# Two graph layers on one core: where the loaded pieces of S are laid out by batch, and who sums the third group's scores

## The chip, the core and the metric

The kernel runs on one core of a Trainium2 chip. Its time is the device time of one execution in microseconds (us), measured several times; below that is compared as a median. A separate execution under the hardware profiler gives the busy times and waits of each engine. The engines are TensorE (PE; its weight loads are PEld), VectorE (DVE), ScalarE (ACT), GpSimd (POOL) and SyncE (SP, which here only issues transfers). All data are float32.

## The reference

There are 16 batches of 1024 nodes with 256 features, and one adjacency matrix `adj` of 1024 x 1024 whose entries are zero except at the edges. Layer 0 is an attention over all nodes with `adj` as a bias. Layer 1 uses `adj` as a weight:

```python
pre_u = jnp.einsum('bud,dk->buk', h_t, W1[:d])
pre_v = jnp.einsum('bvd,dk->bvk', h_t, W1[d:])
hidden = jax.nn.relu(pre_u[:, :, None, :] + pre_v[:, None, :, :] + b1)
S = jax.nn.sigmoid(jnp.einsum('buvk,ko->buvo', hidden, W2)[..., 0] + b2[0])
a_t = jnp.einsum('buv,bud->bvd', S * A_a, h_t)
m_t = jnp.einsum('uv,bud->bvd', A_m, h_t) * h_t
z_t = beta1 * h_t + beta2 * (jnp.einsum('bvd,de->bve', a_t, Wa) + ba) + beta3 * (jnp.einsum('bvd,de->bve', m_t, Wm) + bm)
```

Both `A_a` and `A_m` are `adj`. Since `S` is multiplied by `adj`, its value is needed only at the edges.

## The kernel before

The 16 batches are cut into three groups of 5, 5 and 6 (`GROUPS`; `SIZE[g]` is a group's number of batches). The work has these stages:

1. Layer 0, batch by batch, up to about 1260 us: attention on TensorE (`attend`, L1067), and the two ends of layer 1's edges (`end`, L1105), stored to DRAM as `pu_d` and `pw_d` by node, with the batches of a group side by side. `ha_d` holds h times Wa in the same way. Lists of the edges are made meanwhile.
2. The scores of a group (`scores`, L1279). The edges stand in 135 slots of 128. For a slot GpSimd fetches rows by index (`fetch`, L1226 for `gv`, L1219 for `gu`), VectorE compares them (`compare`, L1255, two instructions a slot), and the result is summed over 272 columns for each batch (`sums`): either by VectorE in one reduction (L1266) or by ScalarE with one accumulating instruction for each batch (L1269). After every part of up to 16 slots ScalarE makes the tanh (`gates`, L1277), VectorE adds one (L1296), and GpSimd scatters each slot's values to `sa_d` in DRAM (`scatter`, L1235): there the batches of a group stand side by side for each pair of nodes. `gv` has 6 buffers in the third group. The first two groups' scores run beside layer 0; the third group's run from about 1330 to 1890 us.
3. The messages of layer 1 (`message`, `product`: L1165, L1185) and, from 1416 us on, the gathers: for a group, a column block `vc` and a row block `c` (8 each), a piece of 128 x 128 pairs is loaded from `sa_d` (`load_sa`, L1339, issued by SP, 7 buffers), laid out by batch by ScalarE (`part_sa`, L1352, tile `apart`, 4 buffers), weighed with `adj` by VectorE in place (`weigh_sa`, L1357), and multiplied with `ha` by TensorE into PSUM (`gather`, L1370, one product for each batch, in two instructions each). The groups are gathered in the order second, first, third, each in 16 halves of four pieces; the messages of the last batches stand between the halves. After a column block VectorE adds the bias (`add_bz`, L1387) and the PSUM result (`finish_z`, L1393), and ScalarE's queue issues the store (`store_z`, L1397).

The third group's gathers can begin only when its scores are all scattered. Each of its six-batch gathers takes its sixth matrix from a tile of its own (`st["rest"]`).

The order of the work on each engine is fixed by a timetable (`Timetable`): every step has a planned time, the steps are emitted in the order of these times, and each engine then runs its instructions in that order. TensorE's steps follow each other with a planned time of 4/2400 us a column; other steps are placed around them. `begins[p]` is the planned start of the gather of piece p, and

```python
        times.at(due, lambda p=p: load_sa(*p))
        times.at(begins[p] - 8.2, lambda p=p: part_sa(*p))
        times.at(begins[p] - 6.0, lambda p=p: weigh_sa(*p))
```

places the copy 8.2 and the weighing 6.0 planned us before it. The load of a piece is planned 4.0 us before the gather seven pieces earlier. In `scores`, the last argument says for which slots the sums are VectorE's: it is true in the third group for every eighth slot (17 of 135), and false otherwise.

Of the kernel before, what the change touches and what calls it, by code (L numbers as in the profile page):

```python
# [10 lines left out]
ALU = mybir.AluOpType  # L11
# [3 lines left out]
P = 128  # L15
# [356 lines left out]
def edge_layers(  # L372
# [36 lines left out]
    nc = tc.nc  # L409
# [3 lines left out]
    NG = len(GROUPS)  # L413
    SIZE = [hi - lo for lo, hi in GROUPS]
# [508 lines left out]
    st = {}  # L923
# [291 lines left out]
    def fetch(g, k):  # L1215
        t, s = SLOTS[k]
        if s == 0:
            gu = st["gu", t] = pools["gath", g].tile([P, SIZE[g] * R], F32, name="gu", bufs=2)
            nc.gpsimd.indirect_dma_start(  # L1219
                out=gu,  # L1220
                out_offset=None,
                in_=pu_d[g],
                in_offset=bass.IndirectOffsetOnAxis(ap=key_u[:, t : t + 1], axis=0),
            )
        gv = st["gv", k] = pools["gath", g].tile([P, SIZE[g] * R], F32, name="gv", bufs=GV[g])
        nc.gpsimd.indirect_dma_start(  # L1226
            out=gv,
            out_offset=None,
            in_=pw_d[g],
            in_offset=bass.IndirectOffsetOnAxis(ap=idx_v[:, t, s : s + 1], axis=0),  # L1230
        )

    def scatter(g, lg, i, k):
        t, s = SLOTS[k]
        dma = nc.gpsimd.indirect_dma_start(  # L1235
            out=sa_d[g],
            out_offset=bass.IndirectOffsetOnAxis(ap=idx_s[:, t, s : s + 1], axis=0),
            in_=lg[:, i, : SIZE[g]],
            in_offset=None,
            bounds_check=N * N - 1,  # L1240
            oob_is_err=False,
        )
        tc.declare_no_dep(dma.ins, group=f"sa{g}", reason="edges of their own")
        tc.add_to_no_dep_group(f"sa{g}", dma.ins)
# [4 lines left out]
    def compare(k, half):  # L1249
        if k in [0, *PARTS] and half == 0:  # L1250
            st["lg"] = dense.tile([P, PARTS[0], MOST], F32, name="lg", bufs=5)
        cols, op = ((slice(0, HALF), ALU.max), (slice(HALF, R), ALU.min))[half]
        mv = by_batch(st["gv", k])[:, :, cols]
        mu = by_batch(st["gu", SLOTS[k][0]])[:, :, cols]
        nc.vector.tensor_tensor(mv, mv, mu, op)  # L1255

    def place_of(k):

        part = next(i for i, end in enumerate(PARTS) if k < end)
        return (PARTS[part - 1] if part else 0), PARTS[part]  # L1260

    def sums(k, js, lg):
        one = by_batch(st["gv", k])
        i = k - place_of(k)[0]
        if len(js) == one.shape[1]:
            nc.vector.tensor_reduce(lg[:, i, : len(js)], one, AX.X, ALU.add)  # L1266
        else:
            for j in js:
                nc.scalar.activation(  # L1269
                    one[:, j, :], one[:, j, :], AF.Copy, accum_out=lg[:, i, j : j + 1]  # L1270
                )

    def gates(g, k, lg):

        k0, k1 = place_of(k)
        part = lg[:, : k1 - k0, : SIZE[g]]
        nc.scalar.activation(part, part, AF.Tanh, bias=b2_h, scale=0.5)  # L1277

    def scores(g, start, end, on_vector):  # L1279

        for k in range(len(SLOTS)):
            time = start + k * (end - start) / len(SLOTS)

            def first(k=k):
                for n in range(AHEAD[g]) if k == 0 else ():
                    fetch(g, n)
                if k + AHEAD[g] < len(SLOTS):
                    fetch(g, k + AHEAD[g])
                for _ in range(min(len(late), 2 if len(late) > PARTS[0] - 4 else 1)):
                    late.pop(0)()  # L1290

            def last(k=k):
                k0, k1 = place_of(k)
                lg = st["lg", k0]
                part = lg[:, : k1 - k0, : SIZE[g]]
                nc.vector.tensor_scalar(part, part, 1.0, None, ALU.add)  # L1296
                late.extend(lambda i=i: scatter(g, lg, i, k0 + i) for i in range(k1 - k0))

            times.at(time - (15.0 if k == 0 else 0.0), first)
            times.at(time + 0.1, lambda k=k: compare(k, 0))  # L1300
            times.at(time + 0.9, lambda k=k: compare(k, 1))
            k0, k1 = place_of(k)
            if k == k0:
                times.at(time + 0.2, lambda k0=k0: st.update({("lg", k0): st["lg"]}))
            summed = lambda js, k=k, k0=k0: sums(k, js, st["lg", k0])
            if on_vector(k):
                times.at(time + 1.7, lambda f=summed: f(range(SIZE[g])))
            else:
                for j in range(SIZE[g]):
                    times.at(time + 2.0 + 0.6 * j, lambda f=summed, j=j: f((j,)))  # L1310
            if k + 1 == k1:
                times.at(time + 5.4, lambda k=k, k0=k0: gates(g, k, st["lg", k0]))
                times.at(time + 6.0, last)
        ended = end + 4.0
        if g + 1 == NG:
            times.at(ended, lambda: [late.pop(0)() for _ in range(len(late))])
        return ended


    def room(g):  # L1320
        return pools["last" if g + 1 == NG else "late"]
# [13 lines left out]
    def load_sa(g, vc, c):  # L1335

        n = SIZE[g]
        sat = st["sat", g, vc, c] = room(g).tile([P, P, n], F32, name="sat", bufs=SA)
        nc.sync.dma_start(  # L1339
            out=sat.rearrange("p v g -> p (v g)"),  # L1340
            in_=sa_d[g].rearrange("(c p v) g -> c p (v g)", p=P, v=N)[
                c, :, vc * P * n : (vc + 1) * P * n
            ],
        )

    def part_sa(g, vc, c):

        sat = st.pop(("sat", g, vc, c))
        apart = st["apart", g, vc, c] = room(g).tile(
            [P, SIZE[g], P], F32, name="apart", bufs=4  # L1350
        )
        nc.scalar.copy(apart.rearrange("p g v -> p v g"), sat)  # L1352

    def weigh_sa(g, vc, c):
        apart = st["apart", g, vc, c]
        a = adj_sb[:, c, vc * P : (vc + 1) * P]
        nc.vector.tensor_tensor(  # L1357
            apart, apart, a.unsqueeze(1).to_broadcast([P, SIZE[g], P]), ALU.mult
        )

    def gather(g, vc, c):
# [108 lines left out]
    times = Timetable()  # L1470
# [199 lines left out]
    begins = {}  # L1670
# [18 lines left out]
    paced = [started[0] + n * (due - started[0]) / NG for n in range(NG)]  # L1689
    paced[NG - 1] = (paced[NG - 1] + started[NG - 1]) / 2  # L1690
    paced = [max(pair) for pair in zip(started, paced)] + [due]
    for g in range(NG):
        ended = scores(g, paced[g], paced[g + 1], lambda k, g=g: g + 1 == NG and k % 8 == 3)
    opened = paced[NG - 1] + 7.0
    assert lead < paced[NG - 1] - 16.0 and opened < when[0], (lead, paced, when[0])
    times.at(
# [19 lines left out]
    for n, (g, c) in enumerate((g, c) for g in order for c in range(C)):  # L1716
# [4 lines left out]
        else:  # L1721
            k, c1 = divmod(n - HA, C)
# [3 lines left out]
    for i, p in enumerate(parts):  # L1726
        due = when[0] - 36.0 + 4.0 * i if i < SA else begins[parts[i - SA]] - 4.0
        if p[0] + 1 == NG:
            due = max(due, ended + 0.1 + 0.01 * i)
        times.at(due, lambda p=p: load_sa(*p))  # L1730
        times.at(begins[p] - 8.2, lambda p=p: part_sa(*p))
        times.at(begins[p] - 6.0, lambda p=p: weigh_sa(*p))
    for i, (g, vc, half) in enumerate(halves):
        if half == 0:
            due = when[0] - 20.0 + 8.0 * i if i < 4 else when[i - 2] + 13.0
# [6 lines left out]
@with_exitstack  # L1742
def tile_graph_layers(ctx: ExitStack, tc: tile.TileContext, *args):
    nc = tc.nc
    I32 = mybir.dt.int32
    hold = ctx.enter_context(tc.tile_pool(name="hold", bufs=1))
    flag = hold.tile([1, 1], I32, name="flag")
    edge_layers(tc, *args, flag)
    over = nc.values_load(
        flag[0:1, 0:1],  # L1750
        min_val=0,
        max_val=1,
        skip_runtime_bounds_check_because="it is a comparison's result",
    )
    with tc.If(over > 0):
        dense_layers(tc, *args)
# [43 lines left out]
```

## Time and profile before

| what | value |
| --- | --- |
| time, median of 3 runs | 2081.45 us (2078.31 to 2083.23) |
| the profiled execution's own time | 2079.83 us |
| its span, first to last instruction | 2078.1 us |
| granted TensorE clock | 0.994 of full speed |
| busy: PE, DVE, ACT, POOL | 97%, 75%, 66%, 55% of the span |
| `part_sa` L1352 | 192 instructions, 264.2 us of ScalarE |
| `weigh_sa` L1357 | 192 instructions, 165.9 us of VectorE |
| `sums` on VectorE L1266 | 17 instructions, 31.5 us |
| `sums` on ScalarE L1269 | 2058 instructions |

How the lines are read. A group's line has the source line, the engine, the operation, the tiles written and read with their shapes (partitions x elements), the count, then after the first bar the busy time in us and the mean ns of one, and after the second bar the idle time of the engine just before them with what ended it. A line of waits has "who waited <- for whom: us in total, times, longest us". A line of stretches has the start and end in us, the length, then for each engine its busy time and (x) the number of instructions, the granted clock, the transfers' share and GB/s. A line of the timeline has start, duration, engine, line, operation and, in brackets, the idle time before it. An answer on one source line gives duration in ns as least/median/most.

### The profile page before, as it was taken

What the parts mean: (1) busy time and instruction counts of PE and PEld (TensorE: products, weight loads), DVE (VectorE), ACT (ScalarE), POOL (GpSimd) and SP (SyncE); (2) the same over time, 40 slices, a digit from 0 to 9 for tenths busy, and PEclk for the clock granted to TensorE, in tenths of its full rate; (3) what the DMA queues carried; (4) which work ended last, traced back from release to release, by engine and by line L of the source; (5) the groups of instructions that cost most, each with busy time, mean ns of one, the idle gap of its engine ahead of it and who ended that gap; (6) DMA issues with size and microseconds to landing.
All of it is one profiled execution on the core that took longest, in us unless ns stands there. A gap on an engine that the chain in (4) does not pass through costs nothing.

```text
span 2078.1 us, 28958 instructions
## 1 busy us (share of the span) xinstructions
PE 2020.4 (97%) x8577; PEld 1554.9 (75%) x8577; DVE 1566.8 (75%) x2348; ACT 1371.5 (66%) x4842; POOL 1142.4 (55%) x974
## 2 busy tenths in 40 slices
PE   8999999999999999999999999899999999999998
PEld 6888887777786868677888886457677667767887
DVE  7798883677777777677878886578888888884554
ACT  4212222577777868587888777577888888885654
POOL 1121221267676777677777777666777677683000
PEclk9999999999999999999999999999999999999999
DMA  6689886788888889789999999999999999996873
GB/s 220 240 311 343 306 323 235 247 268 288 285 273 270 275 288 297 254 299 308 315 297 318 327 308 310 326 401 399 399 400 370 415 414 405 400 383 254 281 230 123
DMA packets 250007, 644.37 MB, mean 310 GB/s; under 512 B 38642, under 2 KB 139762, under 8 KB 247794
## 3 DMA queue, kind: packets, MB, share of 16 engines
q0 software_dynamic: 82016, 348.87, 47.9%
q1 hardware_dynamic: 132002, 259.36, 34.2%
q10 hardware_dynamic: 35824, 34.22, 4.7%
q8 instruction: 69, 1.13, 0.2%
q14 instruction: 96, 0.79, 0.1%
HBM read 479.56 MB, written 162.92 MB: 309 GB/s over the span
## 4 chain that ended last, share of the span: by engine, by line
PE 61%; DVE 11%; DMA 9%; ACT 8%; issue 7%; POOL 3%; ACTq 0%; POOLq 0%; DVEq 0%
PE pv L1067 18%; PE pp L1105 10%; PE pm L1165 10%; PE pzg L1370 6%; DMA gv<-pw_d,idx_v 5%; ACT gv L1269 5%; PE pf L1013 5%; DVE gv L1255 4%; PE pea L1133 4%; PE pzh L1370 3%; PE pz L1185 2%; ACT apart L1352 2%; POOL sa_d L1235 2%; DMA xh<-in_x_dram 1%; POOL gv L1226 1%
## 5 line engine op out<-in xcount | busy, mean ns | idle before, releaser
L1269 ACT ACTIVATE gv<-gv 128x272 f32<-128x272 f32 x2058 | 856.3, 420 | 313.0 <-DVE gv L1255 204.7
L1255 DVE TENSOR_TENSOR gv<-gv,gu 128x680 f32<-128x680 f32 (+1 forms) x810 | 705.8, 909 | 97.5 <-DMA gv<-pw_d,idx_v 95.5
L1226 POOL DMA_INDIRECT gv<-pw_d,idx_v x405 | 497.1, 1227 | 297.9 <-ACT gv L1269 181.5
L1235 POOL DMA_INDIRECT sa_d<-lg,idx_s x405 | 504.1, 1245 | 135.2 <-issue 108.2
L1067 PE MATMUL pv<-feats,eT 128*128 128x257 f32 x2048 | 465.5, 380 | 2.7 <-DVE eT L1054 2.0
L1165 PE MATMUL pm<-adj_sb,xh 128*128 128x512 f32 x1024 | 452.8, 595 | 2.6 <-DVE xh L1081 2.6
L1067 PEld LDWEIGHTS pv<-feats,eT 128*128 128x128 f32 x2048 | 382.9, 190 | 61.8 <-DVE eT L1054 4.2
L1269 ACT ACTIVATION_READ_ACCUMULATOR gv<-gv 128x1 f32 x2058 | 389.7, 189 | 0.0
L1370 PE MATMUL pzg<-ha_g,apart 128*128 128x256 f32 x1536 | 367.5, 382 | 19.0 <-DVE apart L1357 18.5
L1165 PEld LDWEIGHTS pm<-adj_sb,xh 128*128 128x128 f32 x1024 | 194.3, 191 | 222.4 <-issue 219.8
L1370 PEld LDWEIGHTS pzg<-ha_g,apart 128*128 128x128 f32 x1536 | 290.2, 191 | 77.2 <-DVE apart L1357 29.5
L1352 ACT COPY apart<-sat 128x640 f32<-128x640 f32 (+1 forms) x192 | 264.2, 1394 | 78.0 <-PE pzh L1370 35.5
L1357 DVE TENSOR_TENSOR apart<-apart,adj_sb 128x640 f32<-128x640 f32 (+1 forms) x192 | 165.9, 867 | 123.3 <-ACT apart L1352 123.0
L1105 PE MATMUL pp<-wuv,hT 128*128 128x272 f32 x1024 | 250.5, 395 | 6.7 <-ACT end L1119 3.8
L1105 PEld LDWEIGHTS pp<-wuv,hT 128*128 128x128 f32 x1024 | 194.7, 191 | 53.7 <-issue 6.5
L1054 DVE SCALAR_TENSOR_TENSOR eT<-row,col,grown 128x512 f32<-128x512 f32 x256 | 182.8, 745 | 27.5 <-ACT col L1000 26.8
L852 POOL DMA_INDIRECT table_d<-rec,at x52 | 57.4, 1105 | 248.4 <-DVE rec L845 151.8
L1098 ACT COPY hT<-ph 128x512 f32<-128x512 f32 x96 | 55.1, 575 | 101.0 <-PE ph L1087 100.7
L1133 PE MATMUL pea<-wa,hT 128*128 128x256 f32 x512 | 121.0, 379 | 0.0
L1185 PE MATMUL pz<-wm,mT 128*128 128x256 f32 x512 | 115.7, 379 | 0.0
L1013 PE MATMUL pf<-w1T,xT 128*128 128x257 f32 x512 | 114.1, 380 | 0.9 <-DVE xT L971 0.9
L1370 PE MATMUL pzh<-ha_g,apart 128*128 128x256 f32 x384 | 114.2, 379 | 0.0
(179 smaller groups left out, 1589.0 us busy)
## 6 DMA issues: line engine op xcount, KB each, us to landing
sa_d<-zero SPq DMA_DIRECT2D x128, 512.0 KB, 5.6
sat<-sa_d SPq DMA_DIRECT2D x128, 320.0 KB, 9.5
sat<-sa_d SPq DMA_DIRECT2D x64, 384.0 KB, 4.2
pu_d<-end SPq DMA_DIRECT2D x64, 272.0 KB, 4.3
pw_d<-end SPq DMA_DIRECT2D x64, 272.0 KB, 5.8
ha_d<-ea SPq DMA_DIRECT2D x64, 256.0 KB, 4.9
zb_d<-zb ACTq DMA_DIRECT2D x64, 256.0 KB, 7.8
xh<-in_x_dram SPq DMA_DIRECT2D x15, 1024.0 KB, 13.6
```

Source lines behind the costliest of these rows:

```text
L1013: nc.tensor.matmul(pfs[i], lhsT=st["xT"][:, h, c * P : (c + 1) * P], rhs=w1T[:, h, :], start=(h == 0), stop=(h == H - 1),)
L1054: nc.vector.scalar_tensor_tensor(st["eT", b, k, n][:, i, :], st["row"][:, cols], st["col"][:, j : j + 1], grown[:, j, cols], ALU.max, ALU. ...
L1067: nc.tensor.matmul(pv[:, : D + 1], lhsT=st["eT", b, k, j // 4][:, j % 4, i * P : (i + 1) * P], rhs=st["feats", b][:, j, :], start=(j == 0) ...
L1105: nc.tensor.matmul(pp[:, k, :R], lhsT=st["hTi", b, i][:, h, k * P : (k + 1) * P], rhs=wuv[:, side, h, :], start=(h == 0), stop=(h == H - 1),)
L1133: nc.tensor.matmul(pp[:, k, :], lhsT=st["hTi", b, i][:, h, k * P : (k + 1) * P], rhs=wa[:, h, :], start=(h == 0), stop=(h == H - 1),)
L1165: nc.tensor.matmul(pm, lhsT=held[b][:, c, h * P : (h + 1) * P], rhs=adj_sb[:, c, span], start=(c == 0), stop=(c == C - 1),)
L1226: nc.gpsimd.indirect_dma_start(out=gv, out_offset=None, in_=pw_d[g], in_offset=bass.IndirectOffsetOnAxis(ap=idx_v[:, t, s : s + 1], axis=0),)
L1235: dma = nc.gpsimd.indirect_dma_start(out=sa_d[g], out_offset=bass.IndirectOffsetOnAxis(ap=idx_s[:, t, s : s + 1], axis=0), in_=lg[:, i, : ...
L1255: nc.vector.tensor_tensor(mv, mv, mu, op)
L1269: nc.scalar.activation(one[:, j, :], one[:, j, :], AF.Copy, accum_out=lg[:, i, j : j + 1])
L1352: nc.scalar.copy(apart.rearrange("p g v -> p v g"), sat)
L1370: nc.tensor.matmul(st["pzg", g, vc][j // 4][:, j % 4, :], lhsT=apart[:, j, :], rhs=ha, start=(c == 0 and j % 2 == 0), stop=(c == C - 1 and ...
```

## The change

The step `part_sa` goes away. `weigh_sa` takes the loaded piece, in which the batches of a group are the innermost dimension, reads it by batch (so with a step of 5 or 6 floats from one element to the next), multiplies it with `adj` and writes `apart` in order. It is planned 6.6 us before the gather, where the copy was planned 8.2 and the weighing 6.0 us before it. The tile `apart` is now first written by VectorE, and the loaded piece `sat` is released by it. In the third group all slots' sums go to ScalarE.

```diff
-    def part_sa(g, vc, c):
+    def weigh_sa(g, vc, c):
 
         sat = st.pop(("sat", g, vc, c))
         apart = st["apart", g, vc, c] = room(g).tile(
             [P, SIZE[g], P], F32, name="apart", bufs=4
         )
-        nc.scalar.copy(apart.rearrange("p g v -> p v g"), sat)
-
-    def weigh_sa(g, vc, c):
-        apart = st["apart", g, vc, c]
         a = adj_sb[:, c, vc * P : (vc + 1) * P]
         nc.vector.tensor_tensor(
-            apart, apart, a.unsqueeze(1).to_broadcast([P, SIZE[g], P]), ALU.mult
+            apart,
+            sat.rearrange("p v g -> p g v"),
+            a.unsqueeze(1).to_broadcast([P, SIZE[g], P]),
+            ALU.mult,
         )
...
     for g in range(NG):
-        ended = scores(g, paced[g], paced[g + 1], lambda k, g=g: g + 1 == NG and k % 8 == 3)
+        ended = scores(g, paced[g], paced[g + 1], lambda k: False)
...
-        times.at(begins[p] - 8.2, lambda p=p: part_sa(*p))
-        times.at(begins[p] - 6.0, lambda p=p: weigh_sa(*p))
+        times.at(begins[p] - 6.6, lambda p=p: weigh_sa(*p))
```

## The prediction

> **What bounds the kernel now.** I read the page's busy shares first, then stretches of time, then what TensorE waits for, then rows for single instructions.
>
> ```profile
> PE 2020.4 (97%) x8577; PEld 1554.9 (75%) x8577; DVE 1566.8 (75%) x2348; ACT 1371.5 (66%) x4842; POOL 1142.4 (55%) x974
> ```
>
> TensorE is busy 97% of the span; only 58 us of 2078.1 are idle. The change touches nothing before the third group's scores, so I look at the stretch from the first gather (L1370) to the end of these scores, and at the one after it:
>
> ```profile
> core 0: us, PE busy (x) PEld busy (x) DVE busy (x) ACT busy (x) POOL busy (x), PEclk, DMA share, GB/s
> 1410.00:1885.00 475.00, 456.01 (x1797) 332.51 (x1796) 402.49 (x465) 407.04 (x1361) 341.44 (x251) 1.00 1.00 391
> 1895.00:2070.00 175.00, 175.00 (x812) 154.07 (x811) 89.71 (x92) 97.42 (x64) 0.00 (x0) 1.00 0.73 245
> ```
>
> In the first, TensorE idles 19 us of 475, while VectorE and ScalarE are both some 85% busy and the transfers are full. In the second, TensorE has no idle time: nothing done there can gain, and VectorE has 85 us to spare. In the first stretch, the waits are:
>
> ```profile
> PE pzg L1370 <- DVE apart L1357: 18.5, 23, 2.9
> DVE apart L1357 <- ACT apart L1352: 43.4, 40, 5.5
> DVE gv L1255 <- DMA gv<-pw_d,idx_v: 15.7, 9, 4.3
> DVE lg L1296 <- ACT lg L1277: 12.9, 6, 6.2
> DVE zb L1195 <- PE pz L1185: 1.0, 1, 1.0
> ```
>
> So what there is to gain is 18.5 us at most, all of it TensorE waiting for the weighed piece; behind that VectorE waits for ScalarE's copy. VectorE's sum closes: 402.5 busy + 43.4 for copies + 29.6 for the rest = 475.5.
>
> **The change, part by part.** The rows, one shape each:
>
> ```profile
> L1352 ACT COPY apart<-sat 128x640 f32<-128x640 f32 x128 | 166.8, 1320 | 0.8 <-PE pzh L1370 0.8
> L1352 ACT COPY apart<-sat 128x768 f32<-128x768 f32 x64 | 97.4, 1541 | 77.2 <-PE pzh L1370 34.6 <-DMA sat<-sa_d 23.1 <-DVE apart L1357 19.4
> L1357 DVE TENSOR_TENSOR apart<-apart,adj_sb 128x640 f32<-128x640 f32 x128 | 104.7, 822 | 43.7 <-ACT apart L1352 43.4
> L1266 DVE TENSOR_REDUCE lg<-gv 128x6 f32<-128x1632 f32 x17 | 31.5, 1851 | 0.3
> ```
>
> *Removed from ScalarE:* 192 copies, 264 us; of these 126 (164 us) lie in the first stretch, the last 64 (97 us) where TensorE is full, worth nothing.
> *Moved to ScalarE:* 17 reductions become 17x6 = 102 sums. Sums follow each other every 0.41 us in the timeline (starts at 1500.27, 1500.68, 1501.09), so 42 us in all; the 14 reductions inside the stretch make 84 sums, 34 us. ScalarE goes from 407 to 407 - 164 + 34 = 277 of 475 us: no bound any more.
> *Removed from VectorE:* 14 x 1.85 = 25.9 us in the stretch.
> *Added to VectorE:* the weighing now reads its first operand with a step of 5 floats (20 bytes), or 6 in the third group. No row has a tensor_tensor with such a read, so I bound it. From below: no extra cost, 0.82 us as now (the row's 640 elements take 0.15 us + 640 x 1.04 ns). No reason admits a gain: the same count passes. The nearest VectorE row is a small reduction that reads with a step of 9 floats, beside one that reads in order:
>
> ```profile
> L795 DVE TENSOR_REDUCE end<-short x1: 271/271/271, 68.9 to 68.9; 128x9 f32<-128x63 f32 x1
> L762 DVE TENSOR_REDUCE pieces<-reach x1: 258/258/258, 58.2 to 58.2; 128x9 f32<-128x99 f32 x1
> ```
>
> 99 elements in order take 258 ns, so 63 would take 258 - 36 x 1.04 = 220; the strided one takes 271: 0.8 ns more for each element. The nearest large row is ScalarE's own copy, which writes with a step of 128 floats: (1541 - 1320)/128 = 1.73 ns an element, where its copies in order cost (1001 - 575)/512 = 0.83 (L969 and L1098, 1024 and 512 elements): twice. So the extra per piece of 640 lies between 0, 0.51 us (640 x 0.8) and 0.667 us (a second cycle each). I take 0.667, 1.49 us a piece: the row of like size says exactly double, and the small one errs low if some of its start is hidden. From above, a third cycle would add another 0.667.
>
> [...]
>
> *The sum for the stretch.* VectorE: 402.5 - 25.9 + 127 x 0.667 = 461.3 us, in place of 402.5; TensorE needs 456. The waits for the copy (43.4) go. The other 29.6 stay or shrink: ScalarE's tanh (12.9) will come earlier. All kept: 461.3 + 29.6 = 490.9, that is +16 on 475; none kept: 461.3, -14. With the small row's price VectorE needs 441.6, and the ends are -4 and, by TensorE's own 456, -19.
>
> To place it between -14 and +16 I look where VectorE has no room, since its order is fixed and work cannot move from a full stretch to a loose one:
>
> ```profile
> 1425.00:1575.00 150.00, 133.51 (x154) 1.00 1.02 395
> 1600.00:1650.00 50.00, 46.18 (x53) 1.00 1.03 413
> 1725.00:1850.00 125.00, 113.04 (x130) 1.00 1.02 395
> ```
>
> (VectorE busy.) With 40, 15 and 36 weighings and 5, 2 and 4 reductions in them, they become 133.5 - 9.25 + 26.7 = 151.0, 46.2 - 2.5 + 10.0 = 53.7 and 113.0 - 7.4 + 24.0 = 129.6: over by 1.0, 3.7 and 4.6, together 9.3 us; 6.0 us of waits for other things than the copy lie there, of which I keep half: 12.3. In the rest of the stretch VectorE keeps room (1650 to 1725 comes to 63 of 75 us); there TensorE idled 9.2 us, and with the copy gone I give back half: -4.6. Net +7.7, taken as +8.
>
> *New waits on VectorE.* It now waits itself for the piece to land and for TensorE to free one of four apart buffers (ScalarE's 0.8 us in the first stretch). In a run of gathers TensorE takes 2.16 us each, so the buffer is free 3 x 2.16 = 6.5 us before the gather, and the weighing is due 6.6 before: 0.1 us. Queued behind such a wait are the compares, behind them ScalarE's sums, behind them the gv buffers that GpSimd's fetches need. One transfer (ACT gv <- sat, 6.5 us, once) will hold VectorE instead. SP's load of the next piece waits for the weighing's end, due at -6.6 + 1.49 = -5.1 against the copy's -8.2 + 1.32 = -6.9; the load is due at -4.0, so nothing moves unless VectorE is over 1.1 us late. GpSimd's queue is moved past nothing; ScalarE's stores stand behind fewer instructions.
>
> *What I cost at nothing.* ScalarE's 34 us: covered by 198 us of room. GpSimd's 251 issues take 1.36 us here and 0.97 where VectorE stands idle (1886 to 1892): 99 us in excess, which VectorE's instructions seem to cause. With 341 + 53 us of issue it has 80 us of room; that cover goes only if the excess nearly doubles. The last stretch: 89.7 + 64 x 0.8 = 141 of 175 us, so TensorE stays full. Between them:
>
> ```profile
> 1891.21 0.97 POOL L1235 DMA_INDIRECT sa_d<-lg,idx_s  x1 [0.30 <-issue]
> 1893.65 1.27 SPq L1339 DMA_DIRECT2D sat<-sa_d  x3
> 1898.97 0.96 DVE L1357 TENSOR_TENSOR apart<-apart,adj_sb 128x768 f32<-128x768 f32 x1 [3.52 <-ACT apart L1352]
> 1904.50 1.89 PE L1370 MATMUL pzg<-ha_g,apart 128*128 128x256 f32 x8
> ```
>
> The third group's first piece is ready at 1899.9, its gather begins at 1904.5: 4.6 us of cover, 0.8 more without the copy. If the scores do not end earlier, no gain over some 5 us can come through.
>
> **Rivals.** *Faster (full rate):* VectorE needs 376.6, TensorE's 18.5 us of waits fall to some 4 if the scores end earlier with it: -14, 2067. For it: 43.4 us of VectorE's waits go with the copy. Against: both strided rows. The small row's price with a third of the other waits kept (441.6 + 9.9 = 451.5, under TensorE's 456) ends near it. *No change:* double price, but two thirds of the other waits go, as VectorE runs later than whatever it waited for: 461.3 + 9.9 = 471, within 4 us of 475. *GpSimd takes over (slower still):* if its excess doubles, 341 + 99 + 53 = 493, +18, with VectorE's lateness on top +30: 2111. A third cycle an element would be 127 x 1.333 = 169 on VectorE, 546: +71 at least; unlikely. That the change does not do what it says I rule out: both engines' instruction lists change as stated.
>
> **How the numbers follow.** The profiled execution took 2079.83 (span 2078.1), 1.6 under the median of 2081.45; the change in time is put on the median: 2081.5 + 8 = 2089.5. Forecast 0.48 (own range 2086 to 2100), faster 0.26, no change 0.16, GpSimd or a dearer read 0.10. Below 0.2% (4.2 us) a measurement of this kernel cannot tell it from no change. The range runs from 2066 to 2112. Faster 0.26, same 0.16, slower 0.58.
>
> **What would show it.** L1357 near 1.49 us (640) and 1.75 (768): right; near 0.82: the faster rival. VectorE over 95% busy in the first stretch and ScalarE under 60%: right. "PE pzg <- DVE apart" above 18.5 us, near 26: right; below 10: wrong. L1235 and L1226 above 1.6 us: GpSimd's rival. The last stretch should keep its 175 us; if it grows, I have missed a wait there.

## The result, and the profile after

The changed kernel takes 2146.6 us (2142.98 to 2152.64), the kernel before 2081.45: a ratio of 1.032, 95% interval 1.0306 to 1.0334. It is slower, by 65 us. Its profiled execution took 2152.64 us (span 2150.9, clock 0.982). In the changed kernel the weighing is L1353, the gather L1369, the bias L1386, the PSUM sum L1392; the lines of `scores` keep their numbers.

The page's busy shares, then the stretch from the first gather to the end of the third group's scores and the one after it (start and end, length, busy us and instructions of PE, PEld, DVE, ACT and POOL, clock, transfers):

```profile
PE 2044.5 (95%) x8577; PEld 1566.7 (73%) x8577; DVE 1632.6 (76%) x2331; ACT 1179.1 (55%) x4854; POOL 1260.7 (59%) x974
```

```profile
1416.00:1945.00 529.00, 467.34 (x1768) 337.09 (x1768) 430.58 (x443) 304.80 (x1389) 451.36 (x243) 0.95 0.94 348
1972.00:2138.00 166.00, 162.95 (x744) 141.73 (x743) 124.55 (x91) 0.00 (x0) 0.00 (x0) 0.99 0.74 251
```

The last stretch is nearly as full as before (TensorE is busy 163 of 166 us). The first took 475 us and takes 529, and VectorE is no fuller in it (81%, before 85%). TensorE's granted clock is 0.95 there, 1.00 before, and it is busy 467 us instead of 456; but it also idles 62 us, and GpSimd's account below fills the stretch without it. The engine that grew is GpSimd: 341 us for 251 issues before, 451 for 243 now. An issue is here the GpSimd instruction that starts a fetch or a scatter. Its two main groups in the stretch of before:

```profile
L1235 POOL DMA_INDIRECT sa_d<-lg,idx_s x124 | 169.0, 1363 | 38.4 <-issue 32.9 <-DVE gv L1255 1.2 <-DMA gv<-pw_d,idx_v 0.9
L1226 POOL DMA_INDIRECT gv<-pw_d,idx_v x110 | 151.0, 1373 | 87.9 <-ACT gv L1269 61.1 <-issue 16.2 <-ACT apart L1352 4.5
```

Groups of instructions and waits in the stretch of after:

```profile
L1353 DVE TENSOR_TENSOR apart<-sat,adj_sb 128x640 f32<-128x640 f32 x121 | 159.0, 1329 | 0.0
L1235 POOL DMA_INDIRECT sa_d<-lg,idx_s x116 | 235.0, 2026 | 36.2 <-issue 30.5 <-DMA sa_d<-lg,idx_s 1.5 <-DMA gv<-pw_d,idx_v 1.2
L1226 POOL DMA_INDIRECT gv<-pw_d,idx_v x110 | 183.7, 1670 | 36.5 <-issue 28.3 <-DMA sa_d<-lg,idx_s 2.6 <-ACT gv L1269 2.5
```

```profile
ACT gv L1269 <- DVE gv L1255: 154.0, 54, 9.8
DVE gv L1255 <- DMA gv<-pw_d,idx_v: 94.0, 31, 10.2
...
PE pzg L1369 <- DVE apart L1353: 51.9, 29, 5.4
```

The strided weighing costs 1.33 us instead of 0.82 and waits for nothing. A scatter takes GpSimd 2.03 us instead of 1.36, a fetch 1.67 instead of 1.37, and GpSimd hardly waits for another engine any more (2.5 us for ScalarE's sums, 61.1 before): what is left before its issues is nearly all "issue", 0.30 us each. Its 451 us and 243 x 0.30 = 73 fill 524 of 529. VectorE waits 94 us (15.7 before) for the rows that GpSimd fetches late, and behind those compares stand the weighings that TensorE then waits for: 51.9 us instead of 18.5.

From the start of the first gather to the end of the last scatter, two events that the trace dates in every kernel, the sum closes. Before, 1416.0 to 1892.2; after, 1422.3 to 1965.9:

```profile
1963.66 0.97 POOL L1235 DMA_INDIRECT sa_d<-lg,idx_s  x1 [0.31 <-issue]
1964.94 0.97 POOL L1235 DMA_INDIRECT sa_d<-lg,idx_s  x1 [0.30 <-issue]
```

(A stretch of the timeline, GpSimd's last two issues of after.) The window grew from 476.2 to 543.6 us, its start came 6.3 later (it scatters between 1412.5 and 1424.0 in the kernels below that ran where before takes 2080 us), and what follows the last scatter took 185.9 and 185.0: 67.4 + 6.3 - 0.9 = 72.8, the difference of the two spans. The time of this kernel is the end of the last scatter and 185 us.

This table has that window for all kernels below, worked out from their traces: its length, VectorE's busy time in it, the mean and the longest GpSimd issue, and GpSimd's issues with 0.30 us added to each. Some 253 issues lie in every window (189 in half_scatter).

| kernel | ratio to before (95%) | window us | VectorE us | issue mean, longest us | GpSimd with 0.30 each, us |
| --- | --- | --- | --- | --- | --- |
| before | 1 | 476.2 | 399 | 1.36, 6.0 | 421 |
| after | 1.032 (1.0306 to 1.0334) | 543.6 | 434 | 1.83, 13.6 | 539 |
| only_stride | 1.0314 (1.026 to 1.0369) | 546.0 | 459 | 1.82, 14.0 | 538 |
| only_sums | 0.9975 (0.9966 to 0.9985) | 467.3 | 376 | 1.32, 5.8 | 412 |
| one_input | 1.0031 (1.0019 to 1.0042) | 484.2 | 432 | 1.56, 7.8 | 468 |
| half_scatter | 1.0176 (1.0149 to 1.0204) | 506.1 | 431 | 2.18, 14.7 | 468 |
| weigh_twice | 1.0307 (1.0287 to 1.0328) | 538.6 | 500 | 1.28, 2.2 | 402 |
| stride_out | 1.01 (1.0083 to 1.0116) | 498.7 | 421 | 1.64, 11.9 | 489 |
| split | 1.0264 (1.0244 to 1.0285) | 536.0 | 442 | 1.79, 18.9 | 529 |
| stride_pe | 1.0004 (0.9985 to 1.0024) | 469.4 | 372 | 1.33, 8.9 | 411 |
| extra_step1 | 1.0131 (1.0052 to 1.021) | 503.4 | 458 | 1.22, 2.2 | 384 |
| extra_step2 | 1.0135 (1.0055 to 1.0216) | 504.0 | 458 | 1.22, 2.2 | 384 |
| extra_step4 | 1.0238 (1.0158 to 1.0318) | 527.0 | 489 | 1.28, 4.8 | 399 |
| extra_step5 | 1.026 (1.0171 to 1.035) | 527.6 | 489 | 1.27, 3.8 | 394 |
| extra_free1 | 1.0155 (1.0113 to 1.0196) | 515.5 | 450 | 1.54, 8.1 | 466 |
| extra_free5 | 1.0273 (1.0236 to 1.0311) | 536.2 | 478 | 1.67, 10.8 | 497 |
| after_gap | 0.9999 (0.9988 to 1.0011) | 476.6 | 453 | 1.38, 2.8 | 425 |
| mix_half | 0.9933 (0.9913 to 0.9953) | 461.1 | 375 | 1.34, 8.7 | 416 |

Ratios are to runs of the kernel before on the same chip; where the extra_step kernels and extra_free1 ran, it took 2103 to 2105 us.

### The profile page after: what moved, and what is told of

Its sections match the earlier page's. It is cut to its first block, busy times and chain, and to the rows that moved or that the text cites. A ratio compares the mean times of both kernels' runs of the same rounds, so it can differ in the third digit from the quotient of the medians.

```text
span 2150.9 us, 28917 instructions
## 1 busy us (share of the span) xinstructions
PE 2044.5 (95%) x8577; PEld 1566.7 (73%) x8577; DVE 1632.6 (76%) x2331; ACT 1179.1 (55%) x4854; POOL 1260.7 (59%) x974
## 4 chain that ended last, share of the span: by engine, by line
PE 55%; DMA 15%; DVE 10%; issue 9%; POOL 7%; ACT 3%; POOLq 0%; SPq 0%; DVEq 0%; ACTq 0%
PE pv L1067 16%; PE pm L1165 10%; DMA gv<-pw_d,idx_v 9%; PE pp L1105 8%; PE pzg L1369 5%; PE pf L1013 4%; DVE gv L1255 4%; PE pea L1133 4%; POOL sa_d L1235 3%; POOL gv L1226 3%; PE pz L1185 2%; PE pzh L1369 2%; ACT gv L1269 2%; DVE apart L1353 2%; DMA sa_d<-lg,idx_s 2%
## 5 line engine op out<-in xcount | busy, mean ns | idle before, releaser
L1269 ACT ACTIVATE gv<-gv 128x272 f32<-128x272 f32 x2160 | 898.4, 419 | 467.6 <-DVE gv L1255 301.5
L1255 DVE TENSOR_TENSOR gv<-gv,gu 128x680 f32<-128x680 f32 (+1 forms) x810 | 707.9, 911 | 185.9 <-DMA gv<-pw_d,idx_v 181.4
L1226 POOL DMA_INDIRECT gv<-pw_d,idx_v x405 | 526.7, 1301 | 256.1 <-ACT gv L1269 131.9
L1235 POOL DMA_INDIRECT sa_d<-lg,idx_s x405 | 579.9, 1432 | 134.6 <-issue 111.3
L1165 PE MATMUL pm<-adj_sb,xh 128*128 128x512 f32 x1024 | 457.6, 600 | 13.1 <-DVE mT L1176 9.0
L1369 PE MATMUL pzg<-ha_g,apart 128*128 128x256 f32 x1536 | 381.4, 393 | 55.2 <-DVE apart L1353 52.2
L1269 ACT ACTIVATION_READ_ACCUMULATOR gv<-gv 128x1 f32 x2160 | 407.7, 189 | 0.0
L1369 PEld LDWEIGHTS pzg<-ha_g,apart 128*128 128x128 f32 x1536 | 297.8, 196 | 120.1 <-DVE apart L1353 72.6
L1353 DVE TENSOR_TENSOR apart<-sat,adj_sb 128x640 f32<-128x640 f32 (+1 forms) x192 | 265.4, 1399 | 50.2 <-PE pzh L1369 31.2
L1219 POOL DMA_INDIRECT gu<-pu_d,key_u x63 | 88.7, 1409 | 65.1 <-PE pv L1067 41.0
L1369 PE MATMUL pzh<-ha_g,apart 128*128 128x256 f32 x384 | 117.2, 388 | 0.0
```

The lines of the kernel that those rows point to most:

```text
L1165: nc.tensor.matmul(pm, lhsT=held[b][:, c, h * P : (h + 1) * P], rhs=adj_sb[:, c, span], start=(c == 0), stop=(c == C - 1),)
L1226: nc.gpsimd.indirect_dma_start(out=gv, out_offset=None, in_=pw_d[g], in_offset=bass.IndirectOffsetOnAxis(ap=idx_v[:, t, s : s + 1], axis=0),)
L1235: dma = nc.gpsimd.indirect_dma_start(out=sa_d[g], out_offset=bass.IndirectOffsetOnAxis(ap=idx_s[:, t, s : s + 1], axis=0), in_=lg[:, i, : ...
L1269: nc.scalar.activation(one[:, j, :], one[:, j, :], AF.Copy, accum_out=lg[:, i, j : j + 1])
L1353: nc.vector.tensor_tensor(apart, sat.rearrange("p v g -> p g v"), a.unsqueeze(1).to_broadcast([P, SIZE[g], P]), ALU.mult,)
L1369: nc.tensor.matmul(st["pzg", g, vc][j // 4][:, j % 4, :], lhsT=apart[:, j, :], rhs=ha, start=(c == 0 and j % 2 == 0), stop=(c == C - 1 and ...
```

## The experiments

The expectations call theories by letters. G: GpSimd's issues, held up by VectorE, pace the stretch. R (the moved sums) and S (VectorE's own time) are the first rivals to it. P, fitted to the first four runs: the stretch lasts as long as VectorE's instructions with two operands in SBUF and some 0.40 us for each of GpSimd's issues; the "port" in its name is the author's guess at a cause, and no run shows one. T: the step of the access itself holds GpSimd; the "line" in extra_step1's expectation is likewise an assumption that no run shows. N, which the last runs test, is explained at its place.

### One half of the change each

**only_stride**: the changed kernel, with the 17 reductions left on VectorE.

```diff
-        ended = scores(g, paced[g], paced[g + 1], lambda k: False)
+        ended = scores(g, paced[g], paced[g + 1], lambda k, g=g: g + 1 == NG and k % 8 == 3)
```

> The strided weighing alone; the 17 reductions of the third group stay on VectorE. Theory G (GpSimd's queue is the bound: its transfers' issues are held while VectorE runs instructions with two operands in SBUF, and the longer weighing holds them more): GpSimd's issues stay at 1.75 to 1.9 us in the stretch of gathers and scores, the time is 2130 to 2150 us. Theory R (what cost the time is that all sums are ScalarE's, so that the compared rows come free later): issues fall to some 1.4 us, time 2080 to 2095 us. Theory S (VectorE's own longer busy time): slower than the changed kernel by the 26 us of reductions that come back, 2160 to 2175 us.

**only_sums**: the same edit the other way round, in the kernel before.

> The sums alone: ScalarE makes the copy as before and all sums of the third group; VectorE weighs in place as before. G: VectorE loses 17 instructions with one operand, GpSimd's issues stay within 0.1 us of 1.36, time 2078 to 2092 us (ScalarE goes from 407 to some 441 of 475 us). R: 2110 to 2140 us.

only_stride takes 2145.0 us, as long as the whole change; only_sums takes 2074.9, less than either kernel. So the weighing's half of the change makes the whole loss, and the moved sums are a small gain of their own.

### Less of the suspected load

**one_input** makes the layout on VectorE with the same strided read, but with one operand (a reduction over an axis of length 1); it leaves out the product with `adj`.

```diff
-        nc.vector.tensor_tensor(
...
+        nc.vector.tensor_reduce(
+            apart, sat.rearrange("p v g -> p g v").unsqueeze(3), AX.X, ALU.add
+        )
```

> The strided weighing is replaced by a reduction over a dimension of one element: the same strided read of the piece, the same 640 or 768 results in order, but no second operand (the product with adj is left out). The instruction is expected to take within 0.15 us of 1.33 us. G: GpSimd's issues fall below the 1.36 us of before, to 1.1 to 1.3 us, and the time to 2062 to 2085 us. If it is the stride that disturbs GpSimd, or VectorE's own time (S): issues stay near 1.86 us, or the time stays at 2130 to 2150 us.

**half_scatter**: the changed kernel without every second slot's scatter in the third group.

```diff
     def scatter(g, lg, i, k):
+        if g + 1 == NG and k % 2:
+            return
```

> The changed kernel, but every second slot of the third group is not scattered (67 of GpSimd's issues left out, and their values with them). G: GpSimd's queue loses 67 x 2.3 us = 154 us in the stretch and is no bound any more: time 2070 to 2095 us. S or R: GpSimd is not the bound, time 2130 to 2150 us.

one_input's instruction is as long as the strided weighing, and almost the whole loss is gone (2085.5 us), though the issues, at 1.56 us, stay longer than the 1.1 to 1.3 us that G expected. From its groups of instructions:

```profile
L1353 DVE TENSOR_REDUCE apart<-sat 128x640 f32<-128x640 f32 x124 | 162.3, 1323 | 0.4 <-DMA sat<-sa_d 0.4
```

So neither VectorE's time (432 us in the window, 434 in after) nor the strided read alone is the cause; that the instruction reads two operands matters. half_scatter won half the loss back (2116.9 us), which no theory had said: GpSimd had 64 issues fewer, and those left became longer (2.18 us).

### Two-operand time, the side of the step, shorter instructions, the step on TensorE

**weigh_twice**: the kernel before with the in-place weighing made twice, so that `adj` goes in squared.

```diff
+        nc.vector.tensor_tensor(
+            apart, apart, a.unsqueeze(1).to_broadcast([P, SIZE[g], P]), ALU.mult
+        )
```

> The kernel before with the weighing issued twice, in order and in place (the output then holds adj squared): no stride on VectorE, only more time in instructions with two operands in SBUF. Theory P (port: the stretch lasts as long as VectorE's time in two-operand instructions plus some 0.40 us for each GpSimd issue, whatever the stride; in the runs so far 376.6 + 251 x 0.39 = 475 before, 430.6 + 243 x 0.41 = 529 changed, 432.9 + 188 x 0.39 = 507 with half the scatters): 376.6 + 99 + 100 = 576, 101 us more than before, 2165 to 2195 us, and GpSimd's issues rise above 1.8 us. Theory T (the step in the read disturbs GpSimd): issues stay near 1.36 us. If VectorE's busy time alone is the bound: 402.5 + 99 and 30 of other waits, 2110 to 2145 us.

**stride_out**: the changed kernel, reading `sat` in order and writing `apart` with a step of 128 floats.

```diff
-            apart,
-            sat.rearrange("p v g -> p g v"),
-            a.unsqueeze(1).to_broadcast([P, SIZE[g], P]),
+            apart.rearrange("p g v -> p v g"),
+            sat,
+            a.unsqueeze(2).to_broadcast([P, P, SIZE[g]]),
```

> As the changed kernel, but VectorE reads the piece in order and writes apart with a step of 128 floats. If a strided write costs VectorE what a strided read does (1.3 us): P and T both say 2135 to 2155 us. If it is free (0.82 us): P says 376.6 + 100 = 477 us for the stretch and, with ScalarE relieved, 2065 to 2082 us. T says the same.

**split**: the changed kernel, each weighing cut into two instructions, of two batches and of the rest.

```diff
+        for lo, hi in ((0, 2), (2, SIZE[g])):
...
+                apart[:, lo:hi, :],
+                by[:, lo:hi, :],
+                a.unsqueeze(1).to_broadcast([P, hi - lo, P]),
```

> The changed kernel with each weighing cut into two instructions, two batches and then the rest. P: VectorE gains some 0.1 us a piece, 13 us in the stretch, and nothing is freed: 2150 to 2175 us. If instead GpSimd is let in at the end of an instruction (theory E), more ends mean shorter issues: below 1.65 us on the mean, 2100 to 2130 us.

**stride_pe**: no layout at all: VectorE weighs in order, and TensorE takes its columns with a step of 5 or 6 floats.

```diff
-                lhsT=apart[:, j, :],
+                lhsT=apart[:, :, j],
```

> No layout by batch at all: VectorE weighs the piece in order, without ScalarE's copy, and TensorE takes each batch's matrix from it with a step of 5 or 6 floats as its weights. P: VectorE's weighing is back at 0.82 us, the stretch at 477 us or, TensorE permitting, a little less: 2065 to 2085 us, if the weight load stays at 0.19 us. If the strided load costs twice (0.38 us, where a product starts every 0.216 us): 2048 x 0.16 = 336 us more, some 2400 us.

weigh_twice ends P. Its waits and groups between 1415 and 1880 us:

```profile
POOL gv L1226 <- ACT gv L1269: 124.3, 52, 5.2
...
PE pzg L1373 <- DVE apart L1360: 53.6, 41, 4.1
```

```profile
L1226 POOL DMA_INDIRECT gv<-pw_d,idx_v x101 | 121.2, 1200 | 151.0 <-ACT gv L1269 124.3 <-issue 6.7 <-ACT apart L1352 6.1
```

VectorE is busy 500 of 538.6 us, most of it on two operands, more than in any other kernel here; yet a fetch takes 1.20 us and GpSimd waits 124 us. It is slow because VectorE is full, not GpSimd. stride_out had nearly the changed kernel's instruction length (1.29 us) and lost a third as much: 2101.9 us, where both theories said 2135 to 2155. split shows that the length of the instruction is not the point: pieces of 0.62 and 0.86 us, issues of 1.79; its 2135.2 us lie between what P and E expected. stride_pe is even with before: VectorE back at 0.82 us a piece, no copy, issues 1.33 us; its weight loads pay instead, from 190 to 310 ns, of which little shows in the time: what follows the last scatter takes 190.7 us, 185.9 before (first the group of before, then of stride_pe, in the last stretch):

```profile
L1370 PEld LDWEIGHTS pzg<-ha_g,apart 128*128 128x128 f32 x509 | 96.7, 190 | 13.2
```

```profile
L1366 PEld LDWEIGHTS pzg<-ha_g,apart 128*128 128x128 f32 x501 | 117.5, 310 | 0.0
```

### The price of the step, and whether the step holds GpSimd

**extra_step1, extra_step2, extra_step4, extra_step5**: the kernel before, with one more product of 320 of the weighed elements after each weighing, written over the spent piece, read with a step of s floats.

```diff
+        nc.vector.tensor_tensor(
+            extra.rearrange("p (s v) -> p s v", s=s),
+            flat.rearrange("p (v s) -> p s v", s=s),
+            adj_sb[:, c, :320].rearrange("p (s v) -> p s v", s=s),
+            ALU.mult,
+        )
```

> The kernel before, with one more instruction on VectorE after each weighing: the product of 320 floats of apart with 320 of adj, written over the piece that is no longer needed. Here it reads apart in order. Expected 0.48 us each, VectorE some 54 us busier in the stretch. Theory T (a step of a line or more in VectorE's read holds GpSimd's issues): they stay between 1.25 and 1.4 us; time 2085 to 2115 us. Theory D (it is VectorE's time in instructions with two operands): they rise to 1.45 us or more.

> The same, reading the same 320 floats of apart with a step of 2 floats (8 bytes). T: as in order, 0.48 to 0.6 us each and issues at 1.25 to 1.45 us; time 2085 to 2120 us. D: issues as with step 1.

> The same with a step of 4 floats (16 bytes). T: 0.7 to 0.8 us each, issues at 1.55 us or more; time 2110 to 2150 us. D: issues no higher than its time asks for, within 0.1 us of the run with step 1.

> The same with a step of 5 floats (20 bytes), as the changed kernel has it. T: as step 4, 0.7 to 0.8 us each, issues at 1.55 us or more, time 2110 to 2150 us; if the harm grows with the step, more than step 4. D: within 0.1 us of the run with step 1.

The added product's group in the four kernels: s = 1 and 2 (the same line in both), then 4, then 5:

```profile
L1363 DVE TENSOR_TENSOR sat<-apart,adj_sb 128x320 f32<-128x320 f32 x192 | 94.7, 493 | 6.6
```

```profile
L1363 DVE TENSOR_TENSOR sat<-apart,adj_sb 128x320 f32<-128x320 f32 x192 | 143.6, 748 | 6.6
```

```profile
L1363 DVE TENSOR_TENSOR sat<-apart,adj_sb 128x320 f32<-128x320 f32 x192 | 143.2, 746 | 6.6
```

A step of 8 bytes costs nothing here (493 ns, as in order); at 16 and 20 bytes it costs (748 - 493) / 320 = 0.80 ns an element, which the weighing itself shows too: (1329 - 822) / 640 = 0.79. But all four have issues of 1.22 to 1.28 us, and their ratios (1.0131, 1.0135, 1.0238, 1.026) go with VectorE's added time. T falls.

### Breaks in VectorE's chain

What the slow kernels share shows in the timeline. A stretch of it in the changed kernel, first VectorE, then GpSimd (start, duration):

```profile
1524.03 0.71 DVE L1176 TENSOR_TENSOR mT<-pm,hT 128x512 f32<-128x512 f32 x1
1524.63 1.94 DVE L1255 TENSOR_TENSOR gv<-gv,gu 128x816 f32<-128x816 f32 x2
1526.46 1.36 DVE L1353 TENSOR_TENSOR apart<-sat,adj_sb 128x640 f32<-128x640 f32 x1
1527.71 1.96 DVE L1255 TENSOR_TENSOR gv<-gv,gu 128x816 f32<-128x816 f32 x2
1529.54 2.62 DVE L1353 TENSOR_TENSOR apart<-sat,adj_sb 128x640 f32<-128x640 f32 x2
```

```profile
1525.23 7.70 POOL L1226 DMA_INDIRECT gv<-pw_d,idx_v  x1 [0.30 <-issue]
1533.23 1.01 POOL L1235 DMA_INDIRECT sa_d<-lg,idx_s  x1 [0.30 <-issue]
```

Each of VectorE's seven instructions from 1524.63 on starts some 0.1 us before the one ahead of it ends (1526.46 against 1526.57), so between two of them there is no gap; the chain ends at 1532.16. The fetch issued at 1525.23 ends at 1532.93, 0.77 us after that end. Counted so over the whole windows: a *break* is a place where VectorE's chain of instructions with two SBUF operands stops: a gap, or an instruction with an operand in PSUM or with one operand. An issue is counted as let in at a place if it ends 0.76 to 1.06 us after the VectorE instruction there ends, and as not let in if it goes on longer:

| kernel | at a break | first place without a break | later ones | mean issue us |
| --- | --- | --- | --- | --- |
| before | 62 of 62 | 107 of 114 | 0 of 16 | 1.36 |
| stride_pe | 50 of 50 | 112 of 117 | 0 of 22 | 1.33 |
| weigh_twice | 93 of 93 | 86 of 87 | none | 1.28 |
| extra_step5 | 98 of 98 | 87 of 90 | 0 of 1 | 1.27 |
| after | 69 of 69 | 69 of 113 | 12 of 87 | 1.83 |
| split | 55 of 56 | 73 of 123 | 24 of 163 | 1.79 |

At a break an issue gets in nearly always. Without one it gets in at the first place that it meets or hardly at all, and then waits for the chain's end. In before, VectorE waits for the copy ahead of 40 weighings; in weigh_twice and the extra_step kernels the second of two instructions needs the first, which leaves 0.03 us of gap; in the changed kernel VectorE's instructions mostly wait for nothing and do not depend on each other. That GpSimd's issues are let in for certain only at breaks is theory N, and three runs test it from both sides.

The table shows two differences between before and after, not one. The windows have 119 breaks in before and 87 in after; and at the first place without a break the share let in falls from 107 of 114 to 69 of 113. Lost breaks alone do not make the loss: stride_pe has 91 and keeps the high share.

**after_gap**: the changed kernel with a break behind each weighing, one element multiplied by 1 in place.

```diff
+        one = apart[:, 0, 0:1]
+        nc.vector.tensor_scalar(one, one, 1.0, None, ALU.mult)
```

> The changed kernel with one element of each weighed piece multiplied by 1 in place right after the weighing: an instruction on one operand that depends on the one before it, so that VectorE's unbroken chain of two-operand instructions ends at every weighing. Theory N (GpSimd's issue is let in for certain only where VectorE's chain of two-operand SBUF instructions breaks; in the changed kernel nothing breaks it for 5 to 19 us): the mean issue in the third group's stretch falls from 1.87 us to 1.25 to 1.40, none over about 4.5 us is left, GpSimd's busy time falls from 451 to 310 to 350 us and it waits again; VectorE gains some 127 x 0.15 = 19 us; the time falls from 2145 to 2080 to 2110 us. Rival (the strided read holds GpSimd by what it takes of SBUF, whatever stands between the instructions): the mean issue stays at 1.75 us or more, and the time at 2140 to 2165.

**extra_free5**: extra_step5 without the dependence: the added product reads `adj` only.

```diff
-            flat.rearrange("p (v s) -> p s v", s=5),
+            adj_sb[:, (c + 1) % C, :320].rearrange("p (v s) -> p s v", s=5),
```

> The kernel before with one more VectorE product of 320 floats after each weighing, read with a step of 20 bytes as in extra_step5, but of adj by adj: it does not depend on the weighing, so that no gap stands between the two. It writes over the spent piece and changes no output. Theory N: without the gap the issues are let in less often: mean issue above 1.35 us (extra_step5 had 1.25), tails over 3 us come back; time 2155 to 2180 us on a chip with 2105 for the kernel before, 2130 to 2160 on one with 2080. Rival (a strided read of SBUF does it only in long pieces, or only on a tile that a DMA has written): mean issue 1.20 to 1.30 us and the ratio of extra_step5, 1.017 to 1.035.

**extra_free1**: the same with s = 1.

> As extra_free5, with the added product read in order (0.49 us instead of 0.74): independent of the weighing, no gap, no step. If the missing gap alone keeps GpSimd's issues out, they take 1.5 us or more, as in extra_free5 (1.70). If it needs both, a missing gap and a strided read in the chain (kernels without a strided read let an issue in at the first boundary that it meets in some 95 of 100 cases, gap or not), they take 1.25 to 1.40. Time in both cases by VectorE: ratio 1.008 to 1.025.

after_gap has more VectorE work than the changed kernel and takes 2080.1 us, ratio 0.9999: the whole loss is gone. The stretch of its timeline, VectorE and GpSimd, and the groups between 1415 and 1880 us:

```profile
1605.94 1.34 DVE L1353 TENSOR_TENSOR apart<-sat,adj_sb 128x640 f32<-128x640 f32 x1
1607.32 0.15 DVE L1360 TENSOR_SCALAR apart<-apart 128x1 f32<-128x1 f32 x1
1607.40 1.93 DVE L1255 TENSOR_TENSOR gv<-gv,gu 128x816 f32<-128x816 f32 x2
```

```profile
1606.24 1.88 POOL L1235 DMA_INDIRECT sa_d<-lg,idx_s  x1 [0.31 <-DVE gv L1255]
1608.42 1.73 POOL L1226 DMA_INDIRECT gv<-pw_d,idx_v  x1 [0.30 <-issue]
```

```profile
L1235 POOL DMA_INDIRECT sa_d<-lg,idx_s x119 | 168.5, 1416 | 41.8 <-issue 29.3 <-DVE lg L1296 6.3 <-DVE gv L1255 3.0
L1226 POOL DMA_INDIRECT gv<-pw_d,idx_v x109 | 151.4, 1389 | 74.2 <-ACT gv L1269 42.7 <-issue 17.8 <-DVE gv L1255 6.3
```

The scatter waits through the weighing, which ends at 1607.28, and is done at 1608.12, 0.84 us later, though the compares run on. No issue is longer than 2.8 us, and GpSimd waits for ScalarE again, 42.7 us. Its window has 155 breaks. VectorE is busy 454.5 of 470 us between 1415 and 1885; after_gap has nothing to spare there and does not beat before.

From the other side, taking the gap out of extra_step5 made its issues longer, from 1.27 to 1.67 us, and extra_free1 against extra_step1 from 1.22 to 1.54. So here the missing gap does it without any step (109 breaks in extra_free1, 220 in extra_step1); the step adds to it. Their times moved little (1.026 to 1.0273, 1.0131 to 1.0155, with intervals that overlap): in both GpSimd has room left, and still waits for ScalarE, 41 us in extra_free5 and 46 in extra_free1.

### A version that beats both

**mix_half**: the sums on ScalarE; in the first two groups every second piece as in stride_pe, the others and the third group with the copy.

```diff
+    def plain(g, c):
+        return g + 1 < NG and c % 2 == 1
...
+                lhsT=apart[:, :, j] if plain(g, c) else apart[:, j, :],
```

> A version meant to beat both: all sums of the third group's scores on ScalarE, and of the first two groups' pieces every second one without the copy: VectorE weighs it in order (0.82 us) and TensorE reads its columns with a step of 5 floats (0.309 us a weight load against 0.190); the other pieces and the third group keep ScalarE's copy. Both theories: ScalarE at some 350 us instead of 441 in the stretch, VectorE at 380, GpSimd's issues at 1.3 us; the kernel with the sums alone moved took 0.9975 of before, this one 0.992 to 0.999: 2064 to 2078 us where before takes 2080.

It takes 2067.6 us, ratio 0.9933 (0.9913 to 0.9953), and its profiled run's window is 461 us; TensorE is busy 455.71 of it:

```profile
1424.00:1885.00 461.00, 455.71 (x1801) 356.43 (x1800) 374.58 (x445) 372.80 (x1460) 340.05 (x254) 1.00 1.00 397
```

## Why the prediction was wrong

The sign was right, the size was not: +8 us forecast, +65 measured, above the range's upper end of 2112. The sign was luck: the +8 came from a VectorE that has no room, and with the price that was measured the prediction's own sum puts VectorE at 441 us, under TensorE's 456, and its ends at -4 and -19.

- **The read's price** was too high by a third: 0.667 us forecast for a piece of 640, 0.507 measured. The small reduction's row (0.8 ns an element) was the right neighbour; I chose the copy of another engine, against rows of it that read other tiles (`pt` and `ph`, which TensorE writes). The 1.04 ns an element that stands for one cycle in the prediction is the rate in order of the compares of before (862 ns for 680 elements, 1004 for 816). A third cycle, 1.333 us more for a piece, showed in no run. The runs put the edge between a step of 8 bytes (493 ns for 320 floats) and one of 16 (748), and the price at 0.80 ns an element.
- **VectorE's sum** was close: with the measured price it is 402.5 - 25.9 + 127 x 0.507 = 441, and 431 to 434 was found. It was not the bound: "VectorE over 95% busy" failed: 81%.
- **The step that failed** is GpSimd under "What I cost at nothing". It gave 99 us of excess a cover of 80, to go "only if the excess nearly doubles". It more than doubled: 254 x (1.83 - 0.97) = 218 us by the table's means, and GpSimd, with 539 of 543.6 us, set the length of the window. The trace of before had the sign of it: issues of up to 6.0 us under a VectorE that was only 85% busy. I read the mean, and took the excess for something that grows with VectorE's busy time. It does not: weigh_twice has VectorE busy 500 us and issues of 1.28. It grows when an issue misses the first place and VectorE's chain then goes on without a break. The change does both: it takes away breaks, the waits for the copy (43.4 us in 40 waits) that I had booked as pure gain, and with the strided read more issues miss the first place (44 of 113, 7 of 114 before).
- **The other waits** "stay or shrink": wrong. The compares' wait for fetched rows went from 15.7 to 94.0 us, and TensorE's for the weighed piece to 51.9, not 26.
- **The rival "GpSimd takes over"** named the cause and its mark (L1235 and L1226 above 1.6 us: 2.03 and 1.67), but stopped at a doubled excess, +18 to +30, at a chance of 0.10 together with a dearer read.
- **Right**: ScalarE under 60% (58%); no new wait of VectorE for buffers (0.0 us before L1353); what follows the last scatter hardly changed (185.0 us, 185.9 before). The 4.6 us of cover before the third group's gather did not limit anything.
- **Not separated** in the prediction: the moved sums alone, which gain 0.25%.

With one operand in place of two little of the loss is left (one_input, ratio 1.0031). One point decided here: an issue is not let in at the end of each instruction. One took 13.6 us in after (1665.87 to 1679.50), through a row of instructions of 1.0 to 1.5 us each. By what a two-operand instruction holds an issue up is not shown here.

What stays open: why the first place without a break lets an issue in 107 times of 114 in one kernel and 69 of 113 in another. A strided read in VectorE's chain goes with the low share where instructions also follow without a gap (only_stride, split, extra_free5); stride_pe has few breaks and no strided read on VectorE, and keeps the high share. But extra_free1, without any strided read, comes to 112 of 137, and one_input, whose strided read has one operand, to 21 of 60. One more thing stands in the traces: at a later place without a break, issues were let in right behind a strided instruction (12 of 29 in after, 24 of 86 in split, 11 of 27 in extra_free5, 12 of 37 in only_stride) and hardly ever behind one in order (0 of 58, 0 of 77, 0 of 70, 1 of 65). Nothing here shows how the step does either. In stride_out some 50 issues fit neither rule. Why half_scatter's remaining issues grew longer is not shown either.

## What to carry to other kernels

A wait that is removed from VectorE can have been the moment at which GpSimd's indirect transfers got in (here 43.4 us of waits for the copy went, and the mean issue rose from 1.36 to 1.83 us): before booking it as gain, look in the timeline at the longest issues, not at the mean, and at what stands on VectorE during them. Where GpSimd must issue beside long rows of independent two-operand instructions, a dependent one-element instruction of 0.15 us in each row can be worth more than it costs (after_gap: 18.8 us for 122 of them between 1415 and 1880 us, and the ratio went from 1.032 to 0.9999). And where one late event is followed by a fixed tail, as the last scatter and 185 us here, follow that event rather than the busy shares.

## What the runs showed of the hardware

- A VectorE product read with a step of 4 or 8 bytes took 493 ns for 320 floats (extra_step1, extra_step2), with 16 or 20 bytes 748 and 746 (extra_step4, extra_step5). Written with a step of 512 bytes, a product of 640 floats took 1289 ns (stride_out), against 822 in order (before).
- A GpSimd indirect issue took 0.97 us beside an idle VectorE (the last ones of before and after), and ended some 0.85 us after the place where it was let in (0.77 us in the stretch of after shown above, 0.84 in that of after_gap). VectorE need not stop for it (107 of 114 first places without a break in before), and a gap of 0.03 us was enough (weigh_twice: all 52 issues that met the gap between the two weighings).
- The instruction of one SBUF operand in one_input (the reduction, 1323 ns) let an issue in at its start: 69 of 69 that met one after a compare.
- TensorE's weight loads of 128 x 128 floats took 190 ns in order (before) and some 310 with a step of 5 or 6 floats (stride_pe); behind products of 256 columns most of that was hidden (190.7 us after the last scatter in stride_pe, 185.9 before).
